# Products of x2 with layer 2's weight: by couples of tiles, transposed one couple ahead

## The chip, the cores and the metric

The kernel runs on one core of a Trainium2 chip. The core has a matrix engine (TensorE, PE in the profile), a vector engine (VectorE, DVE), a scalar engine (ScalarE, ACT), GpSimd (POOL) and a sync engine (SP) that here only issues DMAs. Each engine works through its own queue of instructions in a fixed order; semaphores tie the queues together. The metric is the device time in microseconds (us) of one execution; a comparison is made of several executions of each kernel.

## The reference: what is computed

Four layers of a graph network on 4096 nodes with 256 features each. Every layer ends in `x = layernorm(x + layer(x))`. Layer 0 multiplies by the adjacency matrix and a weight; layer 1 has two steps of attention in which each row keeps only its largest weights up to a mass of 0.9; layers 2 and 3 multiply by the adjacency matrix again. The two that meet at the change are the end of layer 1 and layer 2:

```
# layer 1, one step: rows of A keep the top of the softmax, up to a mass of 0.9
Xa = A @ Xa
Z = Z + Xf @ U1[n].T + Xa @ U2[n].T
# layer 2, on x2 = the output of layer 1
support = concatenate((x2, adj @ x2, edge), axis=1)
out = support @ weight + bias
```

`weight` has 513 rows. The kernel writes layer 2 as `adj @ (x2 @ W_b) + x2 @ W_a + ...`, so it first needs, for every row of x2, the product with both halves of the weight: 256 numbers in, 512 out. That product is called zu in the code, and it is what the change concerns.

## The kernel before, in words

The 4096 rows are 32 tiles of 128 rows (NT = 32). Layer 1's second step (n = 1) goes over the tiles one after another. For a tile it computes 4096 logits a row, their exponentials `e`, the threshold of the row, zeroes what lies under it (`settle`), and then multiplies `e` by the features of all nodes (`pieces`: eight groups of four transposes of `e`, line L713, a copy on ACT, L716, and four matmuls, L738).

Rows whose threshold can't be settled by the quick way are put off. They are gathered, 128 at a time, into extra tiles of rows, called jobs. A job's work is a generator, `put_off`, that yields between its stages; `advance(job)` runs one stage. The last stages of a job are: the search for the threshold (`bracket`, `tops`, `pick`), then `flag`, then `settle`. `flag` asks whether any of the 128 rows is still unsettled: a matmul with a column of ones adds up the marks `bad` (L555), ACT copies the sum to an integer (L557), DVE reads it into a register (L614) and branches on it (L615). On the branch not taken DVE goes on at once with three passes of `match_replace` over `e` (L625) and four masked sums (L630), after which `e` is ready for `pieces`.

Two jobs are left when the 32 tiles are done; the code below calls them the first and the second job. `finish(job, last, todo, beside)` runs a job to its end. Work that has nothing to do with the job can be laid beside it: functions in `todo` are called between the stages, functions in `beside` between the groups of the job's `pieces`. That work is the zu of the tiles: half of it beside the first job's `pieces`, half between the second job's stages.

For one tile, `zu_tile` loads 128 rows of x2 from DRAM (SP's queue, L849), `transposed` makes two transposes on PE (L177) and one copy of the transpose on ACT (L179), `zu` makes two matmuls of 128x512 (L840; in the profile each counts as two, since the data are f32) and one copy on ACT (L843), and the result goes to DRAM (L850). In the buffer of rows that is free at that time there is room for four tiles of x2 and four of results. `zu_ps` has two PSUM banks, used in turn; `tr`, into which all transposes go, has two; `xt`, the copy of a transpose, has two buffers.

The order in which each engine gets its instructions is not the order of the Python text alone. The text is traced, and a scheduler then orders each engine's queue by the place in the text, the buffers that are free and its own notion of how long things take. The result is fixed when the kernel is built; on the chip every engine follows it. An `If` such as that of `settle` leaves a jump (L615) in the queue of every engine.

After both jobs a loop `left_over` runs as many times as there are further rows (not at all here), all engines meet, and layers 2 and 3 follow (matmuls of line L167).

Of the kernel before, what the change touches and what calls it, by code (L numbers as in the profile page):

```python
# [48 lines left out]
def gnn_stack(ctx, tc, x, adjt, adjn, w0, b0, w1, w2t, w3t, u1t, u2t, ln_g, ln_b, w2, b2, w3, b3, out):  # L49
# [3 lines left out]
    nc = tc.nc  # L53
    N = x.shape[0]
    NT = N // P
# [67 lines left out]
    def rows(t, it):  # L123
        return t[it * P : (it + 1) * P, :]

    def all_rows(t):
        return t.rearrange("(t p) d -> p t d", p=P)
# [43 lines left out]
    def transposed(*srcs):  # L171

        n = 2 * len(srcs)
        ps = ps_tr.tile([P, 4, P], F32, tag="tr", name="tr")
        for s, src in enumerate(srcs):
            for c in range(2):
                nc.tensor.transpose(ps[:, 2 * s + c, :], src[:, c * P : (c + 1) * P], ident)  # L177
        t = work.tile([P, 4, P], F32, tag="xt", name="xt")
        nc.scalar.copy(t[:, :n, :], ps[:, :n, :])  # L179
        return t  # L180
# [141 lines left out]
    with tc.tile_pool(name="l1", bufs=1, reuse_waits="tile") as l1:  # L322
# [433 lines left out]
        def put(dst, st, t):  # L756

            if "to" in st:
                nc.gpsimd.indirect_dma_start(  # L759
                    out=dst, out_offset=bass.IndirectOffsetOnAxis(ap=st["to"][:, 0:1], axis=0), in_=t, in_offset=None)  # L760
            else:
                nc.sync.dma_start(rows(dst, st["tile"]), t)
# [44 lines left out]
        def after(n, st):  # L807


            def s1():  # L810
                st["h"] = mix(n, st)

            def s2():
                h = st["h"]
                mv, r = ln_stats(h)
                nc.vector.scalar_tensor_tensor(h, h, mv[:, 0:1], cur["g"], op0=ALU.subtract, op1=ALU.mult)
                nc.vector.scalar_tensor_tensor(h, h, r, st["x1"], op0=ALU.mult, op1=ALU.add)
                ln_apply(h, h, ln_stats(h))
                put(x2_d, st, h)
                if "z" in cur and st["tile"] is None:  # L820
                    put(zu_d, st, zu(h))

            return [s1] if n + 1 < STEPS else [s1, s2]

# [6 lines left out]
            cur["z"] = {"w": w, "x": e[:, 4 * D : 8 * D].rearrange("p (k o) -> p k o", o=D),  # L831
                        "out": e[:, 8 * D : 16 * D].rearrange("p (k o) -> p k o", o=2 * D), "n": 0}

        def zu(x):

            z = cur["z"]
            xt = transposed(x)
            ps = ps_acc.tile([P, 512], F32, tag=("acc", "nef")[z["n"] % 2], name="zu_ps", bufs=1)
            for c in range(2):
                nc.tensor.matmul(ps, xt[:, c, :], z["w"][:, c, :], start=(c == 0), stop=(c == 1))  # L840
            out = z["out"][:, z["n"] % 4, :]
            z["n"] += 1
            nc.scalar.copy(out, ps)  # L843
            return out

        def zu_tile(i):

            x = cur["z"]["x"][:, i % 4, :]
            nc.sync.dma_start(x, rows(x2_d, i))  # L849
            nc.sync.dma_start(rows(zu_d, i), zu(x))  # L850

        def take_rows(n, slots, e):

# [59 lines left out]
        def run_step(n, es):  # L913

            later = {"base": spare0}
            tiles = {}
            last = []
            jobs = []  # L920

            def advance(job):

                cur["late"] = True
                st = next(job["stages"], "end")
                cur["late"] = False
                if st == "end":
                    return True
                if st is not None:
                    job["st"] = st  # L930
                return False

            def finish(job, last, todo=(), beside=()):
                while not advance(job):
                    for f in todo[:4]:
                        f()
                    todo = todo[4:]
                for f in todo:
                    f()
                ops = {}  # L940
                for k, f in enumerate(beside):
                    ops.setdefault(k * NLC // len(beside), []).append(f)
                for k, fs in enumerate(last):
                    ops.setdefault(k + 1, []).extend(fs)
                cur["late"] = True
                pieces(n, job["st"], None, ops)
                cur["late"] = False
                return [[f] for f in after(n, job["st"])]

            starts = {min((k + 1) * NT // LATER[n] - 1, NT - 2): k for k in range(LATER[n])}  # L950
            for i in range(-2, NT):
                st = tiles.pop(i, None)
                cd = tiles.get(i + 1)
                nxt = None
                if i + 2 < NT:

                    nxt = {"tile": i + 2, "q": cur["qs"].pop(0), "e": logits_in(es[i % 2]), "later": later, "G": {}}
                    tiles[i + 2] = nxt
                if i + 1 == NT and n == 0:
                    for fs in last:  # L960
                        for f in fs:
                            f()
                    last = []
                    left_over(n, es[NT % 2], later)
                ops = {}

                def at(g, f, *args):
                    ops.setdefault(g, []).append(lambda: f(*args))

                for g, fs in zip((1, 2), last):  # L970
                    for f in fs:
                        at(g, f)
                if 0 < i + 2 < NT - 1:
                    turned = []
                    g = 1 if n else 6
                    at(g - 1, lambda i, turned: turned.append(transposed(cur["xa"][:, i + 3, :])), i, turned)
                    at(g, lambda turned: cur["qs"].append(query(None, turned[0])), turned)
                if cd is not None:
                    peak_groups(cd)
                    at(1, exp_rows, cd)  # L980
                for job in jobs:
                    at(1, advance, job)
                if cd is not None:
                    rounds = 8 if n else KEPT // 8
                    at(2, tops, cd, rounds)
                    at(2, pick, cd, rounds)
                    at(4, flag, cd)
                    if n == 0:
                        for k in range(8):
                            at(4 + k // 2, gather, cd, k)  # L990
                    else:
                        at(5, lambda cd: [None for _ in settle(cd)], cd)
                for job in jobs:
                    if n and i + 1 == NT:
                        at(4, advance, job)
                    at(6, advance, job)
                if i + 1 == NT and n == 0:
                    cur["next"] = load_halves(es[1 - NT % 2], xf_d, nc.sync)
                if i < 0:
                    now = FIRST[n][i + 2]  # L1000
                else:
                    now = [i + 2] if FIRST[n][1][-1] < i + 2 < NT else []
                pieces(n, st, nxt, ops, now)
                last = [[f] for f in after(n, st)] if st is not None else []
                if i in starts:
                    k = starts[i]
                    if len(jobs) > (i == NT - 2):
                        last = finish(jobs.pop(0), last)
                    e = es[NT % 2] if k + 1 == LATER[n] else es[2]
                    jobs.append({"stages": put_off(n, k, e, later)})  # L1010
                    if i < NT - 2:
                        advance(jobs[-1])
            if n == 0:
                for fs in last:
                    for f in fs:
                        f()
                last = []
                cur["late"] = True
                fetch(n, jobs[0]["st"])
                cur["late"] = False  # L1020
                cur["nef_done"] = True
                for i in range(FIRST[1][0][0]):
                    r_product(1, i, cur["next"])
            todo = []
            if n > 0:

                z_room(es[1 - NT % 2])
                todo = [lambda i=i: zu_tile(i) for i in range(NT)]
            for k, job in enumerate(jobs):
                if k + 1 < len(jobs):  # L1030
                    last = finish(job, last, beside=todo[: NT // 2])
                    todo = todo[NT // 2 :]
                else:
                    last = finish(job, last, todo)
            for fs in last:
                for f in fs:
                    f()
            if n > 0:
                left_over(n, es[NT % 2], later)
# [33 lines left out]
    with tc.tile_pool(name="l23", bufs=1, reuse_waits="tile") as l23:  # L1073
# [68 lines left out]
        for it in range(NT):  # L1142
# [5 lines left out]
            last = acc  # L1148
# [49 lines left out]
```

## Time and profile before

| what | value |
|---|---|
| median of 3 runs | 3308.88 us (3306.8 to 3313.18) |
| the profiled execution's own time | 3340.46 us |
| its span | 3338.8 us |
| PE busy over the span | 3024.1 us (91%) |
| DVE, ACT, POOL busy | 2395.2, 1873.3, 781.6 us |
| 2664 to 2713 us, first job's `pieces` with zu beside it | PE busy 47.97 of 49.00 us |
| 2713 to 2756 us, zu between the second job's stages | PE busy 37.62 of 43.00 us |
| 2756 to 2789 us, the second job's `pieces` and its end | PE busy 24.53 of 33.00 us |

Times inside the profile are microseconds from the start of the span. A line of the timeline gives the start, the duration, the engine, the line of the kernel, the operation with what it writes and reads, how many were merged, and in square brackets how long the engine had been idle before it and what ended the wait. The profiled execution is about 1% longer than the median run.

### The profile page before, as it was taken

The numbers are of one execution on the slowest core, as the hardware profiler recorded it, in microseconds if no ns is written. First come the engines' busy times: TensorE is split into PE (matmuls) and PEld (weight loads), VectorE is DVE, ScalarE is ACT, GpSimd is POOL, SyncE is SP. The second block draws the span as 40 slices with busy tenths as digits, with TensorE's granted clock in tenths as the row PEclk, the third lists the DMA queues.
The fourth block names the chain that finished last, engine by engine and source line by source line (L and its number), as shares of the span: only waits on it lengthen the run. The fifth ranks groups of instructions, "written<-read, shape, count | busy, mean of one in ns | idle before, by whom it ended". The sixth has DMA issues, their size and how long they took to land. (4 is left out here: it accounts for less than half of the span.)

```text
span 3338.8 us, 46384 instructions
## 1 busy us (share of the span) xinstructions
PE 3024.1 (91%) x14600; PEld 2462.3 (74%) x14600; DVE 2395.2 (72%) x7120; ACT 1873.3 (56%) x3162; POOL 781.6 (23%) x915
## 2 busy tenths in 40 slices
PE   6999888999999998779998898999999796999998
PEld 5888667777877777557887777877788554888886
DVE  7888858777777777346997888799799683444444
ACT  3555666766766665436555454555465333666664
POOL 1111245656666666100000001000100001000000
PEclk9999999999999998889999999999999898999999
DMA  9888366777777676331000211011111143333332
GB/s 174 139 142 138 71 103 119 134 125 135 135 133 123 122 134 144 94 116 42 25 23 21 32 29 37 28 31 37 29 34 34 32 142 117 114 109 106 100 110 81
DMA packets 247858, 300.17 MB, mean 90 GB/s; under 512 B 34672, under 2 KB 201520, under 8 KB 247600
## 3 DMA queue, kind: packets, MB, share of 16 engines
q0 software_dynamic: 46576, 104.94, 23.1%
q1 hardware_dynamic: 188800, 180.93, 18.7%
q10 hardware_dynamic: 12224, 11.23, 1.1%
q8 instruction: 118, 1.93, 0.3%
q14 instruction: 140, 1.15, 0.2%
HBM read 331.17 MB, written 66.45 MB: 119 GB/s over the span
## 5 line engine op out<-in xcount | busy, mean ns | idle before, releaser
L653 PE MATMUL acc_r<-xh,adjq 128*128 128x512 f32 x2048 | 616.2, 431 | 27.3 <-ACT adjq L650 20.4
L738 PE MATMUL acc_bank<-xa,at 128*128 128x256 f32 x2304 | 569.5, 388 | 29.5 <-ACT at L716 29.0
L639 POOL DMA_INDIRECT G<-x_d,cols x512 | 498.8, 974 | 334.1 <-PE acc_bank L730 155.8
L167 PE MATMUL acc<-xh,a 128*128 128x512 f32 x2048 | 516.5, 405 | 23.1 <-DMA a<-adj_d 15.6
L738 PEld LDWEIGHTS acc_bank<-xa,at 128*128 128x128 f32 x2304 | 424.9, 194 | 91.3 <-ACT at L716 39.9
L650 ACT CAST adjq<-adj 128x512 fp32r<-128x512 uint8 x512 | 315.8, 619 | 307.6 <-PE acc_r L653 95.5
L400 DVE MAX8 cand<-e 128x8 f32<-128x256 f32 x1024 | 381.8, 416 | 138.5 <-ACT e L382 115.2
L653 PEld LDWEIGHTS acc_r<-xh,adjq 128*128 128x128 f32 x2048 | 381.0, 192 | 126.9 <-ACT adjq L650 45.8
L167 PEld LDWEIGHTS acc<-xh,a 128*128 128x128 f32 x2048 | 384.8, 191 | 108.8 <-ACT xh L143 22.7
L382 ACT COPY e<-lg 128x512 f32<-128x512 f32 x552 | 320.2, 586 | 204.4 <-PE lg L381 173.4
L191 POOL TENSOR_TENSOR rstd<-ve,mhalf 128x1 f32<-128x1 f32 x168 | 103.3, 615 | 1377.5 <-DVE ve L189 1332.9
L381 PE MATMUL lg<-kS,q 128*128 128x512 f32 x1104 | 396.1, 444 | 21.0 <-ACT e L382 11.6
L1078 ACT CAST a<-a 128x1024 fp32r<-128x1024 uint8 x256 | 267.8, 1048 | 158.0 <-PE acc L167 121.3
L730 PE MATMUL acc_bank<-G,dg 128*128 128x256 f32 x1024 | 277.1, 392 | 32.8 <-DVE dg L728 13.8
L497 DVE FIND_INDEX8 cols<-top,e 128x8 uint32<-128x4096 f32 x64 | 282.8, 4419 | 0.0
L730 PEld LDWEIGHTS acc_bank<-G,dg 128*128 128x128 f32 x1024 | 194.0, 193 | 82.5 <-DMA G<-x_d,cols 20.3
L167 PE MATMUL acc<-yh,a 128*128 128x512 f32 x1024 | 233.7, 390 | 0.0
L716 ACT COPY at<-at_ps 128x512 f32<-128x512 f32 x296 | 173.8, 589 | 102.5 <-PE at_ps L713 100.8
L252 ACT CAST a<-a 128x1024 fp32r<-128x1024 uint8 x128 | 133.6, 1049 | 156.4 <-PE acc L167 121.4
L167 PEld LDWEIGHTS acc<-yh,a 128*128 128x128 f32 x1024 | 192.1, 188 | 39.7
L381 PEld LDWEIGHTS lg<-kS,q 128*128 128x128 f32 x1104 | 184.5, 194 | 45.2 <-ACT e L382 20.6
L713 PE MATMUL at_ps<-ident,e 128*128 128x128 f32 x1184 | 183.5, 279 | 14.7 <-DVE e L630 14.6
(281 smaller groups left out, 4634.2 us busy)
## 6 DMA issues: line engine op xcount, KB each, us to landing
adj<-adj_d SPq DMA_DIRECT2D x256, 128.0 KB
a<-adj_d SPq DMA_DIRECT2D x256, 128.0 KB
a<-in_adjt POOLq DMA_DIRECT2D x64, 256.0 KB
adj_d<-a SPq DMA_DIRECT2D x64, 256.0 KB
adjn<-in_adjn POOLq DMA_DIRECT2D x64, 256.0 KB
x_d<-x SPq DMA_DIRECT2D x64, 128.0 KB
G<-x_d,cols POOLq DMA_INDIRECT x512
xf_d<-xf_new SPq DMA_DIRECT2D x64, 128.0 KB
```

Of the source, the lines that this page charges most:

```text
L167: nc.tensor.matmul(acc, a[:, j, :], halves(jt), start=(jt == 0), stop=(jt == NT - 1))
L381: nc.tensor.matmul(pl[:, :LC], q[k], kS[:, s], start=(k == 0), stop=(k == 1))
L382: nc.scalar.copy(l[:, s], pl[:, :LC])
L400: nc.vector.max(dst[:, 8 * g : 8 * g + 8], src[:, g * GW : (g + 1) * GW])
L497: nc.vector.max_index(st["at"][:, 8 * r : 8 * r + 8], t8, st["e"][:, :N])
L639: nc.gpsimd.indirect_dma_start(out=g, out_offset=None, in_=x1_d, in_offset=bass.IndirectOffsetOnAxis(ap=st["at"][:, k : k + 1], axis=0))
L650: nc.scalar.copy(a, cur["a8"][:, g % 2 * GP : (g % 2 + 1) * GP, :])
L653: nc.tensor.matmul(acc_r, a[:, j, :], xf[:, jt, :], start=(jt == 0), stop=False)
L713: nc.tensor.transpose(ps[:, j, :], e[:, (g * G + j) * P : (g * G + j + 1) * P], ident)
L730: nc.tensor.matmul(acc_a, dg[:, k % 4, :], st["G"][k], start=(k == 0), stop=(k == KEPT - 1))
L738: nc.tensor.matmul(acc_a, ats[g][:, j, :], cur["xa"][:, jt, :], start=(jt == 0), stop=(jt == NT - 1))
L1078: nc.scalar.copy(a, a8)
```

## The change

Tiles of x2 are taken by twos. `zu_pair(k)` loads rows of tiles 2k and 2k+1 in one DMA, transposes both into one `tr` bank with one ACT copy of 128x512, and keeps the result for the next call; then it makes the zu of the couple that the call before had transposed. There are 17 calls for 16 couples: the first only transposes, the last only multiplies. `zu` takes the transpose in place of the rows; the jobs' own rows (`s2`) call `zu(transposed(h))`. Of the calls, 8 go beside the first job's `pieces`, 9 go to the second job, two after each stage (before: 16 tiles and 16 tiles, four after each stage). Nothing else is different.

```diff
-                    put(zu_d, st, zu(h))
+                    put(zu_d, st, zu(transposed(h)))
...
-        def zu(x):
+        def zu(xt):
 
             z = cur["z"]
-            xt = transposed(x)
             ps = ps_acc.tile([P, 512], F32, tag=("acc", "nef")[z["n"] % 2], name="zu_ps", bufs=1)
...
-        def zu_tile(i):
-
-            x = cur["z"]["x"][:, i % 4, :]
-            nc.sync.dma_start(x, rows(x2_d, i))
-            nc.sync.dma_start(rows(zu_d, i), zu(x))
+        def zu_pair(k):
+
+            z = cur["z"]
+            ahead = z.pop("pair", None)
+            if 2 * k < NT:
+                x = z["x"][:, k % 2 * 2 : k % 2 * 2 + 2, :]
+                nc.sync.dma_start(x, all_rows(x2_d[:N, :])[:, 2 * k : 2 * k + 2, :])
+                z["pair"] = transposed(x[:, 0, :], x[:, 1, :])
+            if ahead is not None:
+                for j in range(2):
+                    nc.sync.dma_start(rows(zu_d, 2 * k - 2 + j), zu(ahead[:, 2 * j : 2 * j + 2, :]))
...
                 while not advance(job):
-                    for f in todo[:4]:
+                    for f in todo[:2]:
                         f()
-                    todo = todo[4:]
+                    todo = todo[2:]
...
-                todo = [lambda i=i: zu_tile(i) for i in range(NT)]
+                todo = [lambda k=k: zu_pair(k) for k in range(NT // 2 + 1)]
...
-                    last = finish(job, last, beside=todo[: NT // 2])
-                    todo = todo[NT // 2 :]
+                    last = finish(job, last, beside=todo[: NT // 4])
+                    todo = todo[NT // 4 :]
```

## The prediction

> **What bounds the kernel now.** The page's busy times say that PE is the engine to watch (91% of the span). The chain that ended last can be followed back only to 2789 us, to the jobs' end, so the stretch that the change touches must be read from the windows and the timeline. First the windows; columns after the length are busy us of PE, PE's weight loads, DVE, ACT, POOL, then granted clock, DMA share, GB/s:
>
> ```profile
> 2664.00:2713.00 49.00, 47.97 (x195) 30.11 (x194) 43.08 (x91) 21.34 (x42) 8.16 (x5) 1.00 0.35 119
> 2713.00:2756.00 43.00, 37.62 (x115) 17.78 (x113) 29.69 (x63) 15.78 (x38) 0.00 (x0) 1.00 0.45 153
> ```
>
> Beside the first job PE has next to no gaps; between the second job's stages it loses 5.4 us of 43. PE's timeline shows where:
>
> ```profile
> 2721.91 0.60 PE L177 MATMUL tr<-ident,e 128*128 128x128 f32 x4
> 2723.92 0.19 PE L555 MATMUL mm_bank<-ones_col,bad_l 128*1 128x1 f32 x2 [1.41 <-DVE bad_l L531]
> 2724.04 3.70 PE L840 MATMUL zu_ps<-e,xt 128*128 128x512 f32 x8
> 2727.58 0.60 PE L177 MATMUL tr<-ident,e 128*128 128x128 f32 x4
> 2728.69 3.70 PE L840 MATMUL zu_ps<-e,xt 128*128 128x512 f32 x8 [0.51 <-ACT xt L179]
> 2732.23 0.60 PE L177 MATMUL tr<-ident,e 128*128 128x128 f32 x4
> ...
> 2755.48 1.04 PE L713 MATMUL at_ps<-ident,e 128*128 128x128 f32 x8
> ```
>
> Two tiles go together already. A couple takes 4.65 us (2727.58 to 2732.23). The matmuls need 3.54 (2728.69 to 2732.23), the transposes about 0.44 (where other matmuls follow at once, the next starts 0.43 to 0.44 later, as at 2700.84 and 2701.27); the rest, 0.67 us, is PE waiting for ACT's copy of the transpose. The second line is the one that decides: the `flag` product of the second job stands in the middle of the couples. DVE had the mark ready just before, and then needs a long run until `e` can be used:
>
> ```profile
> 2723.71 0.16 DVE L531 SCALAR_TENSOR_TENSOR bad_l<-left_l,bad_l 128x1 f32<-128x1 f32 x1
> 2725.39 0.24 DVE L621 TENSOR_SCALAR go_l<-upto,left_l 128x24 f32<-128x24 f32 x1 [1.52 <-DVEq L615]
> 2735.33 4.43 DVE L625 MATCH_REPLACE8 e<-match_l,e 128x4120 f32<-128x4120 f32 x1
> 2739.80 1.28 DVE L630 SCALAR_TENSOR_TENSOR e<-e,t_thr_l 128x1024 f32<-128x1024 f32 x1
> 2745.12 0.16 DVE L547 RECIPROCAL sc_l<-kept_l 128x1 f32<-128x1 f32 x1
> ```
>
> From the flag product (2723.92) to the first quarter of `e` (2739.80 + 1.28 = 2741.08) are 17.16 us, all behind the seven couples that PE still has. The job's transposes start at 2755.48, when PE is through, not when `e` is ready. So PE is the bound here, with 14.4 us to spare on DVE's side.
>
> [...] ACT had copied the couple's transposes by 2723.25 (two copies from 2722.60, 0.65 us), yet the matmuls behind the flag product started at 2724.04, after it. [...] The trace has it at the first job's start, after 6.49 us idle:
>
> ```profile
> 2636.94 1.94 PE L713 MATMUL at_ps<-ident,e 128*128 128x128 f32 x8 [6.49 <-DVE e L630]
> 2638.75 3.38 PE L738 MATMUL acc_bank<-xa,at 128*128 128x256 f32 x8
> 2641.96 0.60 PE L713 MATMUL at_ps<-ident,e 128*128 128x128 f32 x4
> ```
>
> 5.02 us from the first to the third line; the same three steps at 2755.48 take 3.15 (to 2758.63). A cold start costs 1.9 us.
>
> **The change, part by part.** The built queue of the changed kernel on PE reads, at the end of the couples:
>
> ```
> ... tr x4, zu x4, tr x4, zu x4, tr x4, zu x8, flag product (L555), jump (L615), at_ps x8 (job 2), ...
> ```
>
> *The wait for ACT's copy goes.* A couple's transposes now stand one couple before its matmuls. Losses of PE before, from 2664 on, that this removes: 0.55 at the couple of 2712.74, 0.68 at 2717.26, 1.69 at 2721.91 (with the wait for the flag's mark), 0.67 x 6 = 4.02 after it, and 0.90 at 2673.04, where a transpose waited for ACT behind the exponential; in the new queue the copies before and after the exponential leave PE work at that point. Sum 7.84 us. The couples end at 2755.48 - 7.84 = 2747.6.
>
> *Fewer, larger instructions.* ACT makes one copy of 128x512 (0.59 us) for two of 128x256 (0.65 together, overlapped): nothing, since ACT is busy 15.78 of 43 us. SP issues 16 loads in place of 32; its issues cost 0.32 to 0.40 us and hide behind PE. A load of a couple may start when the couple two before it is transposed, 8 us ahead, so hidden[...].
>
> *The flag product moves behind all couples.* This isn't in the diff; the scheduler does it, for the text's order of stages and calls is the same. L555 waited for DVE until 2723.9 and now also for PE until 2747.6. Behind it on ACT is L557 and on DVE the register load L614, which DVE's queue cannot pass: the three passes and four sums over `e` (20 us) start after PE has finished its last couple, with nothing left for PE to do meanwhile. So: flag product 2747.6; first quarter of `e` + 17.16 = 2764.8; transposes of the job 0.16 later (as at 2636.94, 0.16 after the end at 2636.78) = 2764.9; against 2755.48 that is 9.5 us late. PE has then been idle for 17 us and is cold: + 1.9. Sum **+11.4 us**. The later quarters of `e` come every 1.21 us, a group of `pieces` takes 2.17 and needs half a quarter, so only the first counts.
>
> *After that* the queues of all engines are the same, so the end moves by the same amount: `pieces`, the jobs' last rows, the meeting of the engines, layers 2 and 3. SP's last stores of zu, which in the kernel before ran to 2756.6, end sooner and wait for nobody.
>
> Made against the profiled execution: 3340.46 + 11.4 = 3351.9 us. The median run is 0.9905 of it, so 3308.88 + 11.3 = **3320.2 us**, 0.34% slower. No change can be told from one within about 0.2% (6.6 us).
>
> **Rivals.** *The gain arrives (faster).* If the flag product did not hold up DVE, `e` would be ready at 2741.1 and the job would start when the couples end, at 2747.7: 7.8 us earlier, 3301.2 us. For it: the 4.65 us couples with their repeated 0.51 us waits. Against: the built queue, and the matmuls that stayed behind the flag product at 2724.04. The point from which it decides: the flag product must start by 2755.48 - 17.3 = 2738.2 for no loss, which is 2.4 couples of 3.98 us before the end of the couples; it stands after the last. 0.06.
>
> *Transfers become the pace.* A couple moves 256 KB in and 512 KB out; at 3.98 us that is 193 GB/s, against 153 measured here at a DMA share of 0.45. At 2800 to 2820 us the same queues moved 263 GB/s at 0.86. So there is room, but if landings kept the old pace of 4.65 us for the nine couples left, the couples would end 0.67 x 9 = 6.0 us later, all of it ahead of the flag: + 17.4, 3326 us. 0.08.
>
> *Little moves.* If the cold start and a part of the 17.16 us were hidden by something that I haven't seen, or the run's noise takes it, the time stays within 6.6 us. 0.08.
>
> **How the numbers follow.** The main case has 0.78, and around 3320.2 a spread of some 4 us: the runs before lie 6.4 us apart, and the end of the couples may be 2 to 3 us later if a PSUM or result buffer isn't free in time. The range 3313 to 3328 holds it and the slow transfers, and leaves out the gain. Its own range is 3315 to 3325. Faster 0.06, same 0.08, slower 0.86 (0.78 + 0.08).
>
> **What would show it.** In the profile after: couples about 4.0 us apart with no wait for ACT's copy; the last near 2747.6; the flag product right behind; a PE gap of some 17 us ended by DVE's `e`, L630; L713 and L738 at half speed after it; DVE idle from about 2724 to 2749, ended by the branch L615. I am wrong if the gap is under 10 us, or if couples wait for loads, or if something outside 2640 to 2790 us has moved.

## The result and the profile after

The changed kernel took 3313.36 us (median of 20 runs) against 3308.15 us of the kernel before (20 runs). The ratio is 1.0017, interval [1.0011, 1.0024]: slower by 5.2 us, where 11.3 us were forecast. The time lies inside the range 3313 to 3328 by 0.4 us, and below the main case's own range of 3315 to 3325. Three later comparisons of the same two kernels, told below, gave 1.0032, 1.0029 and 1.0033, which is 10 to 12 us.

The profiled executions can't be compared by their whole span: before it was 3338.8 us, after 3307.6. Layer 1's first step, the same code in both, ended 40 us later in the first of them (the last product of gathered rows, L730, at 1370.1 and 1329.9 us). That is not the change: a later profile of the changed kernel reaches the anchor named next at 2664.05 us, as the kernel before does. So all readings here are distances from one anchor, the first transposes of the first job's `pieces` (2663.77 us before, 2621.73 us after), in front of which no work of PE was changed. From there to the end of the span were 675.0 us before and 685.9 after: 10.8 us more. The kernel before was profiled once, so every distance "over before" in this document rests on that one profile.

The windows of the changed kernel; columns as in the prediction (length, busy us of PE, weight loads, DVE, ACT, POOL, granted clock, DMA share, GB/s):

```profile
2622.00:2671.00 49.00, 48.71 (x203) 31.78 (x201) 42.61 (x89) 22.38 (x37) 11.20 (x5) 1.00 0.38 124
2671.00:2704.00 33.00, 33.00 (x100) 15.70 (x98) 10.56 (x44) 13.38 (x24) 0.00 (x0) 1.00 0.56 186
2704.00:2721.60 17.60, 0.15 (x3) 0.04 (x2) 15.56 (x12) 0.63 (x2) 0.00 (x0) 0.63 0.07 26
```

The change does what it says: while couples run, PE has no gap left (33.00 of 33.00 us; before 37.62 of 43.00). The third row is the price: 17.6 us in which next to nothing but DVE works. PE's timeline has both:

```profile
2689.25 3.60 PE L839 MATMUL zu_ps<-e,xt 128*128 128x512 f32 x8
2692.69 0.60 PE L177 MATMUL tr<-ident,e 128*128 128x128 f32 x4
2693.12 3.60 PE L839 MATMUL zu_ps<-e,xt 128*128 128x512 f32 x8
...
2696.99 7.03 PE L839 MATMUL zu_ps<-e,xt 128*128 128x512 f32 x16
2703.96 0.19 PE L555 MATMUL mm_bank<-ones_col,bad_l 128*1 128x1 f32 x2
2721.68 1.94 PE L713 MATMUL at_ps<-ident,e 128*128 128x128 f32 x8 [17.53 <-DVE e L630]
2723.44 3.11 PE L738 MATMUL acc_bank<-xa,at 128*128 128x256 f32 x8
2726.38 0.60 PE L713 MATMUL at_ps<-ident,e 128*128 128x128 f32 x4
```

A couple takes 3.87 us (2689.25 to 2693.12), with no wait for ACT's copy. Then comes the flag product, right behind the last couple, and a pause of 17.53 us that DVE's masked sum ends. The transposes after it run at half speed (1.94 us for eight, 1.04 before; granted clock 0.50 from 2721.68 to 2723.60 us, and 1.00 from 2755.48 to 2758.63 us before); PE is then called cold below. DVE's timeline shows the other side:

```profile
2682.16 0.16 DVE L531 SCALAR_TENSOR_TENSOR bad_l<-left_l,bad_l 128x1 f32<-128x1 f32 x1
2705.84 0.24 DVE L621 TENSOR_SCALAR go_l<-upto,left_l 128x24 f32<-128x24 f32 x1 [23.51 <-DVEq L615]
...
2720.24 1.28 DVE L630 SCALAR_TENSOR_TENSOR e<-e,t_thr_l 128x1024 f32<-128x1024 f32 x1
```

The mark was ready at 2682.3; DVE then stood 23.51 us before the branch (before: 1.52), because the register it branches on is filled by way of PE's flag product, which was queued behind 21.6 us of products that had nothing to do with it.

### The profile page after: what moved, and what is told of

The parts are those of the page before. It is cut to its first block, busy times and chain, and to the rows that moved or that the text cites. A ratio compares the mean times of both kernels' runs of the same rounds, so it can differ in the third digit from the quotient of the medians.

```text
span 3307.6 us, 46298 instructions
## 1 busy us (share of the span) xinstructions
PE 3006.5 (91%) x14600; PEld 2461.0 (74%) x14600; DVE 2393.8 (72%) x7120; ACT 1874.1 (57%) x3146; POOL 784.4 (24%) x915
## 3 DMA queue, kind: packets, MB, share of 16 engines
q1 hardware_dynamic: 188544, 180.93, 19.1%
## 5 line engine op out<-in xcount | busy, mean ns | idle before, releaser
L738 PE MATMUL acc_bank<-xa,at 128*128 128x256 f32 x2304 | 568.0, 387 | 31.0 <-ACT at L716 30.5
L167 PE MATMUL acc<-xh,a 128*128 128x512 f32 x2048 | 519.4, 407 | 22.2 <-DMA a<-adj_d 16.2
L738 PEld LDWEIGHTS acc_bank<-xa,at 128*128 128x128 f32 x2304 | 425.3, 194 | 92.8 <-ACT at L716 41.3
L167 PEld LDWEIGHTS acc<-xh,a 128*128 128x128 f32 x2048 | 386.5, 192 | 109.6 <-ACT xh L143 21.7
L730 PE MATMUL acc_bank<-G,dg 128*128 128x256 f32 x1024 | 276.8, 390 | 58.3 <-DMA G<-x_d,cols 39.7
L730 PEld LDWEIGHTS acc_bank<-G,dg 128*128 128x128 f32 x1024 | 194.0, 193 | 107.5 <-DMA G<-x_d,cols 53.7
L167 PE MATMUL acc<-yh,a 128*128 128x512 f32 x1024 | 233.7, 390 | 0.0
L167 PEld LDWEIGHTS acc<-yh,a 128*128 128x128 f32 x1024 | 192.1, 188 | 39.7
```

The costliest lines, as they stand in the source:

```text
L167: nc.tensor.matmul(acc, a[:, j, :], halves(jt), start=(jt == 0), stop=(jt == NT - 1))
L730: nc.tensor.matmul(acc_a, dg[:, k % 4, :], st["G"][k], start=(k == 0), stop=(k == KEPT - 1))
L738: nc.tensor.matmul(acc_a, ats[g][:, j, :], cur["xa"][:, jt, :], start=(jt == 0), stop=(jt == NT - 1))
```

## The experiments

**Theory A**: the difference is the place of the flag product in PE's queue, and it is local. The second job starts at whichever is later, the end of the couples or the flag product plus 17.7 us. **Theory B**: PE's pause gives part of its time back elsewhere, so that the profile overstates it. **Theory C**: the changed program is some 5.6 us faster somewhere else. B and C were made to explain why the medians first differed by 5.2 us where the profiles differ by 10.8. Each comparison was made on one chip: the runs below on three of them (numbers 5, 14 and 15), the first comparison on one that isn't on record. This table gathers what the runs below gave; distances in the profiles are in us, from the anchor.

| kernel | couples behind the flag | 2nd job starts | to the end of the span | over before | ratio of times |
|---|---|---|---|---|---|
| before | 7 | 91.7 | 675.0 | | |
| changed | 0 | 99.9 | 685.9 | +10.8 | 1.0017 [1.0011, 1.0024] |
| changed, 2nd | 0 | 99.9 | 685.0 | +10.0 | 1.0032 [1.0021, 1.0042] |
| changed, 3rd | 0 | 99.9 | 682.9 | +7.9 | 1.0029 [1.0018, 1.0040] |
| changed, 4th | 0 | 99.9 | 685.6 | +10.5 | 1.0033 [1.0021, 1.0045] |
| flag five from the end | 5 | 82.4 | 665.5 | -9.5 | 0.9980 [0.9971, 0.9989] |
| the same, 2nd | 5 | 82.4 | 666.7 | -8.3 | 0.9977 [0.9970, 0.9984] |
| flag two from the end | 2 | 92.6 | 678.1 | +3.1 | 1.0004 [0.9995, 1.0012] |
| flag seven from the end | 7 | 90.0 | 673.7 | -1.4 | 1.0002 [0.9990, 1.0014] |
| before, flag last | 0 | 108.5 | 696.1 | +21.1 | 1.0054 [1.0040, 1.0069] |
| changed, PE busy in the pause | 0 | 99.9 | 685.5 | +10.4 | 1.0027 [1.0015, 1.0039] |
| couples, none ahead | 7 (one behind the job's first transposes) | 85.8 | 675.4 | +0.4 | 0.9994 [0.9986, 1.0003] |

### The changed kernel again, three times

No edit.

> The changed kernel once more, nothing left out. In the two profiles so far the stretch from the first job's transposes to the end of the span is 10.8 us longer after the change, but the medians differ by only 5.2 us. Theory A (the flag's place, all of it local): the median difference is 10 to 11 us too and 5.2 was drift between runs. Theory B (give-back): part of PE's 17.5 us pause comes back elsewhere in unprofiled runs; difference 5. Theory C (offset of the build): the changed program is some 5.6 us faster somewhere outside the stretch, whatever the flag does; difference 5.

> The changed kernel a third time, nothing left out. Two comparisons gave 1.0017 [1.0011, 1.0024] and 1.0032 [1.0021, 1.0042], whose intervals only just meet, while both profiles show the stretch 10.0 and 10.8 us longer. Theory A (flag's place, local, 10 to 11 us, ratio 1.0030 to 1.0033): a ratio near 1.003 again. Rival (the profile overstates it, the true cost is about 6 us): near 1.002.

> The changed kernel a fourth time, nothing left out. Ratios so far 1.0017, 1.0032, 1.0029, the first beside runs of before of 3308 us, the others beside 3286 us. Theory A: 1.003. Rival (the cost is smaller where the kernel as a whole runs slower): 1.003 if before is near 3286 us in this comparison too, under 1.0025 if it is near 3308 us.

Measured: 3297.95 us against 3286.18, 3296.0 against 3286.42, and 3351.94 against 3341.13, so 11.8, 9.6 and 10.8 us. Theory A asked for 10 to 11, theories B and C for 5. The three intervals begin at 1.0021, 1.0018 and 1.0021, which is 5.9 us or more, so B and C fall here. The kernel before ran at 3308, 3286 (on two chips) and 3341 us in the comparisons, so its level differs between chips or occasions by more than the change is worth, and only comparisons made together count; the last one, on the slowest ground, gave the highest ratio, so the record shows no smaller cost where the kernel runs slower. In all four profiles the second job starts 99.9 us after the anchor. Up to the first product of layer 2 (L167) they are 10.4, 10.0, 10.6 and 11.2 us over before; the third's smaller 7.9 us arises only behind that, in code that is the same. Why the first comparison showed half is open: its interval only just meets those of the others, and its chip may have been another.

### The flag product five couples from the end

Four calls of `zu_pair` are laid in front of the stages' flag, the rest behind it:

```diff
-                while not advance(job):
-                    for f in todo[:2]:
-                        f()
-                    todo = todo[2:]
+                for c in [1, 1, 1, 1]:
+                    if advance(job):
+                        break
+                    for f in todo[:c]:
+                        f()
+                    todo = todo[c:]
+                else:
+                    while not advance(job):
+                        pass
```

> The changed kernel, with calls of zu_pair laid so that four come before the stages' flag and five after it in the text; in the built queue the flag product then stands in front of the last four couples. Nothing left out. All theories: PE has no gap before the second job's transposes; they start 82.4 us after the first job's (before: 91.7, after: 99.95), the PE clock stays full, so 9.3 us less than before in the profile. Theory A and B: median 9.3 us under before. Theory C: 15 us under before. Rival to all three (couples themselves cost more than they show): no gain over before.

> The kernel of flag_mid a second time (flag product five couples from the end), nothing left out. Its profile had the stretch 9.5 us shorter than before, its median was 6.1 us lower. Theory A: 6 to 10 us under before, faster beyond its interval. Rival (a gain of the couples that isn't real outside the profile): within 3 us of before.

(The first of these texts says that four couples follow the flag; it is five.) PE's timeline of this kernel:

```profile
2667.19 3.60 PE L839 MATMUL zu_ps<-e,xt 128*128 128x512 f32 x8
2670.72 0.19 PE L555 MATMUL mm_bank<-ones_col,bad_l 128*1 128x1 f32 x2
2670.84 0.66 PE L177 MATMUL tr<-ident,e 128*128 128x128 f32 x4
...
2682.95 7.03 PE L839 MATMUL zu_ps<-e,xt 128*128 128x512 f32 x16
2689.82 1.04 PE L713 MATMUL at_ps<-ident,e 128*128 128x128 f32 x8
```

From the flag to the job's transposes are 19.1 us, more than DVE needs, and nothing waits: eight transposes take 1.04 us again. The instructions are those of the changed kernel, in another order on PE and nearly the same on the others; moving one product of 0.19 us turns 10 us lost into 8 to 10 us gained. Medians: 3280.04 against 3286.18 and 3278.68 against 3286.42, 6.1 and 7.7 us faster. Theory C, which asked for 15 us, falls here too: the first interval ends at 0.9971, which is 9.5 us. This kernel is faster than both.

### Two couples, and seven

The same edit with other lists: seven ones and three zeros put the flag two couples from the end, ten zeros and a nine put it seven from the end.

> The changed kernel with the calls of zu_pair laid so that the flag product stands in front of the last two couples. Nothing left out. Theory A: flag 74.9 us after the first job's transposes, the second job's 17.7 us later at 92.6 (before 91.7, changed 99.9, flag_mid 82.4), after a PE pause of 10.4 us, so with the cold start of 1.6 us: 2.5 us over before in the profile, about the same in the median. This is near the point from which the place of the flag decides, put at 2.4 couples. Rival (the flag's place is not what matters, the jump in PE's queue or the number of calls per stage is): like flag_mid or like the changed kernel, not between.

> The changed kernel with all nine calls of zu_pair laid behind the stages' flag in the text; in the built queue the flag product then stands seven couples from the end. Nothing left out. Theory A: now PE gets to the flag product before DVE has the mark (PE at 55.5 us, mark at 60.6 us after the first job's transposes), a pause of 5.1 us in front of it, then seven couples in 26.7 us, which hide the 17.7 us of DVE: the second job at 87.3 us, or up to 1.7 us later if the clock falls in the pause; so 3 to 4 us under before in the profile and in the median, and 5 to 7 us over flag_mid. Rival (the earlier the flag the better): at or under flag_mid.

With two left the second job starts 92.6 us after the anchor, as forecast to the tenth: flag at 74.9, plus 17.7. The profile is 3.1 us over before, the median 2.1 us, and the ratio can't be told from 1. So the place decides by degrees: the result lies between the flag at the end and the flag five couples from it, which the rival (a jump in the queue, or calls per stage) did not allow.

With seven left it was expected 3 to 4 us under before; the profile has 1.4 us under, the median shows no difference. PE's timeline says where the rest went:

```profile
2721.36 3.60 PE L839 MATMUL zu_ps<-e,xt 128*128 128x512 f32 x8
2729.98 0.19 PE L555 MATMUL mm_bank<-ones_col,bad_l 128*1 128x1 f32 x2 [5.02 <-DVE bad_l L531]
2730.10 1.11 PE L177 MATMUL tr<-ident,e 128*128 128x128 f32 x4
2731.01 5.71 PE L839 MATMUL zu_ps<-e,xt 128*128 128x512 f32 x8
2736.55 0.60 PE L177 MATMUL tr<-ident,e 128*128 128x128 f32 x4
```

PE reaches the flag product before DVE has the mark, stands 5.02 us, and is cold after it: the next couple takes 6.45 us from its first transpose to the one after (2730.10 to 2736.55), not 3.87. The second job starts 90.0 us after the anchor, where 87.3 to 89.0 were expected: the miss is that cold start, 2.6 us where at most 1.7 had been allowed. A flag that is too early is thus also wrong: it stops the products in front of which it stands.

### The flag product last in the kernel before

Only the order is changed, by an edge that binds the flag product behind the last zu product:

```diff
-                nc.tensor.matmul(pb[:1, 0:1], st["bad"], ones_col, start=True, stop=True)
+                with tc.issue_after(cur["zu_mm"].ins) if "zu_mm" in cur else ExitStack():
+                    nc.tensor.matmul(pb[:1, 0:1], st["bad"], ones_col, start=True, stop=True)
```

> The kernel before the change, single tiles, with only the flag product of the second job queued behind the last zu product. Nothing left out. Couples end 1 us earlier (no wait for the mark among them), then 17.7 us to the job's transposes, then the cold start: 19 us more than before in the profile. Theory A and C: median 19 us over before. Theory B: some 14 us, since the same pause gives back its 5.6 us.

```profile
2695.59 3.70 PE L841 MATMUL zu_ps<-e,xt 128*128 128x512 f32 x8 [0.51 <-ACT xt L179]
2699.22 0.19 PE L556 MATMUL mm_bank<-ones_col,bad_l 128*1 128x1 f32 x2
2716.89 1.94 PE L714 MATMUL at_ps<-ident,e 128*128 128x128 f32 x8 [17.48 <-DVE e L631]
```

Single tiles, waits of 0.51 us and all, and the same pause of 17.5 us. The median is 19.5 us over before (3305.64 against 3286.18), as theories A and C said. Theory B asked for 14; the interval of 1.0040 to 1.0069 is 13 to 23 us, so this run alone speaks against it but doesn't exclude it. The late flag costs about 20 us in single tiles too; the couples take back about half of it.

### PE kept busy in the pause

Twenty products of 128x512 that nobody reads are queued behind the flag product; they are added, nothing is left out:

```diff
+                if "z" in cur:
+                    wz = cur["z"]["w"]
+                    busy = ps_acc.tile([P, 512], F32, tag="acc", name="busy_ps", bufs=1)
+                    for k in range(20):
+                        nc.tensor.matmul(busy, wz[:, 0, :P], wz[:, k % 2, :], start=True, stop=True)
                 st["nb"] = small("nbad", 1, I32)[:1, :]
```

> The changed kernel with 20 extra products of 128x512 (of the weight with itself, into a PSUM bank that nobody reads) behind the flag product, 20 x 0.86 = 17.2 us, so that PE works through the pause. Nothing left out, the 20 products are added. All theories: the job's transposes start when they did after the change, but at full clock, 1.6 us less from them to the end; so 9.2 us over before in the profile. Theory A: median 9 us over before, 1.6 us under the changed kernel. Theory B: no pause, so nothing is given back: 9 us over before and 4 us over the changed kernel. Theory C: 3.6 us over before.

```profile
2694.69 17.43 PE L560 MATMUL busy_ps<-e 128*128 128x512 f32 x40
2712.28 1.07 PE L718 MATMUL at_ps<-ident,e 128*128 128x128 f32 x8 [0.15 <-DVE e L635]
2713.58 1.99 PE L743 MATMUL acc_bank<-xa,at 128*128 128x256 f32 x8 [0.24 <-ACT at L721]
2715.41 0.60 PE L718 MATMUL at_ps<-ident,e 128*128 128x128 f32 x4
...
2726.17 0.41 PE L177 MATMUL tr<-ident,h 128*128 128x128 f32 x2 [2.30 <-DVE h L196]
...
2727.05 3.57 PE L844 MATMUL zu_ps<-e,xt 128*128 128x512 f32 x4
```

The job starts when it did, now at full clock (1.00 granted from 2712.3 to 2726.0 us): 3.13 us to the next group of transposes, not 4.70. In this profile the 1.57 us are lost again some 15 us later, where after a pause of only 2.30 us the zu of the first job's rows takes 3.57 us (1.99 in the changed kernel). The filling needn't be the cause: two profiles of one and the same kernel differ as much at this place, as the last section shows. The median is 3296.31 against 3297.95 of the changed kernel beside it, 1.6 us less as theory A said, but the intervals of the two ratios overlap for the most part. So whether filling the pause is worth its 1.6 us isn't shown, and this run can't exclude theory B's 4 us over the changed kernel either; B falls by the repeats above.

### Couples without the lookahead

```diff
-            ahead = z.pop("pair", None)
+            ahead = None
             if 2 * k < NT:
...
-                z["pair"] = transposed(x[:, 0, :], x[:, 1, :])
+                ahead = transposed(x[:, 0, :], x[:, 1, :])
             if ahead is not None:
                 for j in range(2):
-                    nc.sync.dma_start(rows(zu_d, 2 * k - 2 + j), zu(ahead[:, 2 * j : 2 * j + 2, :]))
+                    nc.sync.dma_start(rows(zu_d, 2 * k + j), zu(ahead[:, 2 * j : 2 * j + 2, :]))
```

> Couples as in the changed kernel, one load and one copy for two tiles, but multiplied in the call that transposes them (16 calls, none ahead). Nothing left out. In the built queue the scheduler makes transposes of two couples and then their products, and the flag product stands six couples in front of the second job's transposes. Theory A: no pause; ACT's copy is waited for once in two couples in place of once in each, so the second job starts some 4 to 6 us earlier than before, median 4 to 6 us under before. Rival (it is the couple itself, the larger load or copy, that costs): slower than before.

```profile
2664.30 0.19 PE L555 MATMUL mm_bank<-ones_col,bad_l 128*1 128x1 f32 x2 [2.82 <-DVE bad_l L531]
2664.41 8.64 PE L839 MATMUL zu_ps<-e,xt 128*128 128x512 f32 x16
...
2674.26 7.13 PE L839 MATMUL zu_ps<-e,xt 128*128 128x512 f32 x16 [0.33 <-ACT xt L179]
...
2690.01 0.60 PE L713 MATMUL at_ps<-ident,e 128*128 128x128 f32 x4
2690.95 3.70 PE L839 MATMUL zu_ps<-e,xt 128*128 128x512 f32 x8 [0.33 <-ACT xt L179]
...
2694.92 1.89 PE L738 MATMUL acc_bank<-xa,at 128*128 128x256 f32 x8
```

The scheduler fills the wait for ACT with a second couple's transposes; two couples take 8.3 us, and the flag product stands in the midst of them. The median is 3.4 us under before, where 4 to 6 were expected; the ratio 0.9994 [0.9986, 1.0003] can't be told from 1. In the trace PE comes to the flag too early and stands 2.82 us, and the products after it take 8.64 us, not 7.13. The job's first transposes do start at 85.8, 5.9 us earlier than before, but they are not the start of its work: the last couple stands behind them, and the first product of `pieces` (L738) starts 90.7 us after the anchor, against 93.0 before. Of these 2.3 us this profile loses 1.7 again at the zu of the first job's rows (3.66 us, 1.98 before), after a pause of 2.31 us. Couples with one load and one copy thus do not by themselves cost the time of the changed kernel (3.4 us under before here, about 10 over with the lookahead); with the lookahead PE is fed without a break, and the built order with the flag product at the end came with it.

## Why the prediction was right, and where its sizes were off

**The number and the mechanism.** The direction, the path and each of its steps came as forecast. The number of the first comparison didn't: 5.2 us with an interval of 3.6 to 7.9, where the sum gave 11.3. That 3313.36 us still lies in the range is luck, by 0.4 us; the later comparisons, not this one, bear the sum out.

**The wait for ACT's copy goes.** Right. The couples end 82.2 us after the anchor (2703.96); forecast were 83.8. The term was mis-sized by 1.6 us: a couple was put at 3.98 us, and measures 3.87, which makes 1.7 us over sixteen.

**Larger instructions cost nothing.** Right: no couple waits for a load, at 186 GB/s. (The prediction's 193 GB/s for a couple in 3.98 us comes to 198 with 1024 bytes a KB.) The rival of slow transfers falls with it.

**The flag product moves behind all couples.** Right, and the core of it. 17.3 us from the flag to the job's transposes were forecast, 17.7 measured: DVE started 1.88 us after the flag product, not 1.47, after its wait of 23.51 us at the branch. The job is 8.2 us late, not 9.5.

**Cold start.** 1.9 us forecast. From the job's first transposes to the next the changed kernel takes 4.70 us, not 3.15, so 1.57 us more, and 1.5 to 2.0 in its four profiles. (The lines from which the 1.9 was read, at 2636.94, are the start of the last tile's `pieces`, not the first job's, which starts at 2663.77; the size holds all the same. The granted clock was 0.50 there from 2636.9 to 2638.7 us.) To take the same 1.9 us after 17 us of idle was the author's estimate from that one start. Whether a cold start reaches the end in full isn't shown: the run with PE kept busy can't tell.

**The sum.** 11.4 us forecast, 10.8 measured between the two profiles, 7.9 to 10.5 in the three later ones; 9.6 to 11.8 in the three later comparisons of medians, but 5.2 in the first. The mechanism and its price are shown by the runs; what made the first comparison smaller is not.

**The gain as a rival.** It was put at 7.8 us, had the flag not held up DVE. The flag five couples from the end is this case: 6.1 and 7.7 us. The point from which the place decides, 2.4 couples, fits: with two couples behind the flag the second job starts 0.9 us later than before, with five 9.3 us earlier.

## What to carry to other kernels

Where work is filled in beside a chain that goes through several engines, a short instruction of that chain on the filled engine needs its own place: late enough that its input is there, early enough that what follows it on the other engine is still covered. The diff doesn't show where it ends up. In the text of both kernels all calls laid between the second job's stages stand in front of the flag: sixteen tiles after the first four of the stages left, or nine calls after the first five, and the flag in the tenth. In the order built for the kernel before, whose tiles wait for ACT's copy, the flag product stands seven couples from the end; without the lookahead too; with it, it stands behind them all. Why the scheduler chose so isn't on record, only the orders are; so look at the built order. The time that the other engine needs behind the product (here 17.7 us behind a product of 0.19 us) is the number to know before the filling is made denser.

## What the runs showed of the hardware that was not expected

How fast PE works after a short pause is not decided by the length of the pause alone. The kernel with the flag five couples from the end was profiled twice, and at the same place, after the same pause, the zu of the first job's rows took 1.98 us in the first profile and 3.66 in the second:

```profile
2703.77 0.41 PE L177 MATMUL tr<-ident,h 128*128 128x128 f32 x2 [2.30 <-DVE h L196]
...
2704.64 1.98 PE L839 MATMUL zu_ps<-e,xt 128*128 128x512 f32 x4
```

```profile
2697.82 0.41 PE L177 MATMUL tr<-ident,h 128*128 128x128 f32 x2 [2.30 <-DVE h L196]
...
2698.69 3.66 PE L839 MATMUL zu_ps<-e,xt 128*128 128x512 f32 x4
```

In the profile before, the same zu took 1.98 us after 2.31 us idle, and the granted clock was 1.00 from 2769.4 to 2772.5 us. In the same way eight records of L791 took 1.99 us after 3.26 us idle (2605.94 us in the profile before, granted clock 1.00 from 2605.9 to 2608.0 us) and 3.64 us after 3.29 us idle (flag seven from the end). After 4.82 or 4.83 us idle the zu of the second job's rows was slow in all eleven profiles in which it was read, 3.19 to 3.78 us; the granted clock was 0.50 from 2788.9 to 2793.5 us before and from 2756.7 to 2761.5 us in the changed kernel. What decides between fast and slow after 2.30 us, or after about 3.3, no run shows. What a cold start cost differs too: 1.6 us (changed kernel), 1.5 (couples without lookahead, 8.64 against 7.13) and 2.6 us (flag seven from the end).
